# Between layers 1 and 2 of a four-layer Flamingo network: where constants load, in which order the last expert tiles, the sums, the norms and the keys stand

## The chip, the cores and the metric

The kernel runs on one core of one Trainium2 chip. The time is that of one execution on the device, in microseconds (us); the kernel before takes 2595.01 us as the median of three runs (2593.57 to 2595.51). The engines are TensorE (PE; its weight loads are PEld), VectorE (DVE), ScalarE (ACT), GpSimd (POOL) and SyncE (SP, which here only issues transfers).

## What is computed

A batch of 8 sequences of 256 tokens, 512 channels each, float32, goes through four layers. Each layer is `x = x + tanh(g_xattn) * attention(norm(x))`, then `x = x + tanh(g_ffn) * ffn(norm(x))`; attention and FFN are others in each layer. The change lies where layer 1's FFN ends and layer 2's attention begins. Cut to these:

```python
# layer 1, FFN: 64 experts of hidden width 176, 8 of them for each token, and a shared MLP
topk_idx, topk_w = _route(x, router_weight, e_bias)
moe_out = _moe_experts(x, topk_idx, topk_w, w_gate, w_up, w_down)
out = moe_out + _silu(x @ sh_gate) * (x @ sh_up) @ sh_down

# layer 2, attention over channels (per sequence: q = norm(x), k = v = ctx)
scaled = jnp.einsum('bsd,bse->bde', q, k) / sqrt(512)
attn = jax.nn.softmax(scaled, axis=1)
out = jnp.einsum('bde,bse->bsd', attn, v)

# layer 2, FFN: dense, hidden width 2048
h = gelu(x @ proj1.T + proj1_bias)
out = h @ proj2.T + proj2_bias

# layer 3, attention: a scan over time with w = -exp(time_decay), u = time_first
```

## The kernel before

The 2048 tokens are 16 tiles `xt[0..15]` of 128 tokens by 512 channels, held in SBUF for the whole run; four tiles are a block (`TB` = 4, `NB` = 4 blocks of `BLK` = 512 tokens, two sequences of `S` = 256 each). `KC` = 4 is the number of 128-wide pieces of the channels. The kernel is written with a tile framework: each engine runs its instructions in one fixed order, which a scheduler finds from priorities and dependencies when the kernel is built. `behind(one, other, reason)` (L134) only puts an instruction behind another in that order; it adds no wait. `tc.add_manual_dep` with the class `Sync` adds a real wait. Pools of tiles (`t2`, `bp`, `fp`, `wp`) decide which buffer a load must wait for.

*The end of layer 1's FFN* (`middle`). The experts run as a pipeline over tiles of up to 128 gathered token rows (`experts1`, L1421): for each tile the gate and up products, `turn` (L1354: the hidden values are transposed on TensorE and copied back, 128 columns by VectorE, L1360, 48 by ScalarE, L1361), `down` (L1401: the products `ed` with the expert's down weights, a part of 128 rows from `w` and a remainder of 48 rows from `wd`), and an indirect transfer by POOL that adds the result to the tokens' rows in DRAM (L1374, a scatter). There are three such accumulators (`SUMS1` = 3, `acc`). `down` takes two tiles at a time, so that their remainders lie side by side on TensorE. Behind the last tile all five engines load a count (`needing`, L1497) into a register and branch on it (`tc.If`, L1500): the block under it handles experts with too many tokens and isn't run with these inputs. Behind the branch `shared1` (L1157) makes the shared MLP of the last block (tiles 12 to 15): products `shg`, `shu`, `shr` (the gate's and up's remaining 48 columns), Silu on ScalarE, `shT` as two halves (L1174, L1180), and the products `shd`. `combine` (L1522) loads the three accumulators of a tile from DRAM (`more<-acc`, 256 KB each, on SP) and adds them to `xt` on VectorE (L1535). `hidden` holds the VectorE instruction behind which the first tiles' sums are put.

*Layer 2* (`back`). b1 and gb2 (bias rows), and later, behind `xattn2(0)` in the program, constants of layer 3 (`wkv_constants`, L1649: `td`, `tf`, and `w` as an Exp on ScalarE; `place_of`, `run`, `gw` and some more, L1906 to L1949) are loaded and made without a place in the order, so that the scheduler puts them right behind the branch. `L1889` to `L1951` set up: for each of the two sequences of block 0 the sums (`combine`), the load of its keys (`load_kx`, `kxvs`), the norm of its two tiles (`norm_of`: statistics on VectorE, L160 and L163, the root on POOL, L169, the result on VectorE, L179). Behind the first norm stand the four additions of `shd` to tiles 12 to 15 (`last_adds`). `emptied` (L1758) writes empty tables for layer 3. `xattn2` (L1552) makes for each sequence four score products (`s`), a maximum (L1568), Exp (`E`, L1570) and the scaling of the values (L1574), then the products `o` and their addition to `xt`. `step` runs pieces of work for later blocks between these; `ready2` (L1600) makes the norm and the transposes (`tr_f`, copied to `xnT_f` by VectorE L105 and ScalarE L107) for the FFN between the products of the second pair of sequences. `ffn2` (L1618) makes `h2p` (first products, 4 tiles by 4 rounds), Gelu (L1634), and `o2f`; in its first round POOL adds the bias row to `xt` (L1637). Its weights `p` come as 64 tiles of 512 KB on SP.

*The order of transfers on SP* is fixed as well: a load that waits for its buffer holds up all that stand behind it.

## Time and profile before

| | us |
|---|---|
| median of 3 runs | 2595.01 (2593.57 to 2595.51) |
| profiled execution, its time | 2596.3 |
| its span (first to last instruction) | 2594.4 |
| TensorE busy | 2447.8 (94%) |
| VectorE / ScalarE / GpSimd busy | 1276.5 / 643.6 / 902.3 |
| mean granted TensorE clock | 0.979 |
| last expert products end (L1410) | 1409.2 |
| shared products begin (shg) | 1412.56 |
| last scatter issued / first load of a sum | 1412.05 / 1420.78 |
| first scores of layer 2 / second sequence's | 1435.86 / 1447.67 |
| last `o` product of block 1 ends | 1496.87 |
| `h2p`, first product of layer 2's FFN, begins | 1502.58 |

All times within an execution are counted from the start of its span. The views used below: the page's list of busy times; windows (busy time of each engine in a stretch, the clock that TensorE was granted there, and the share and rate of the DMA engines); and timelines of one engine, in which each row gives start, duration, engine, line, operation, `out<-in`, shape, count, and in brackets how long the engine stood idle before it and what ended the wait. A name with q behind it (ACTq, SPq) is the engine's queue: issues of transfers, branches, register work.

### The profile page before, as it was taken

The page shows a single profiled execution, that of the slowest core. Times are in us where ns is not written, and L with a number is a line of the kernel's source. Part 1 is how long each engine was busy: PE and PEld are TensorE (multiplying, and loading weights), DVE is VectorE, ACT ScalarE, POOL GpSimd, SP SyncE. Part 2 cuts the span into 40 slices and gives each one's busy share as a digit, 9 for nine tenths or more (in the row PEclk, how much of TensorE's full clock was granted, in tenths as well). Part 3 has the DMA queues.
Part 4 walks back from the last instruction along what each step waited for, and adds up shares of the span by engine and source line. Part 5 has one row for each costly group of instructions (what it writes and reads, how often), then busy time and mean ns, then how long its engine had stood idle before and what let it go on. Part 6 is the DMA issues. An engine that isn't in the chain of part 4 may idle for free. (4 is left out here: it accounts for less than half of the span.)

```text
span 2594.4 us, 29853 instructions
## 1 busy us (share of the span) xinstructions
PE 2447.8 (94%) x10389; PEld 1258.2 (48%) x10404; DVE 1276.5 (49%) x3517; ACT 643.6 (25%) x1451; POOL 902.3 (35%) x843
## 2 busy tenths in 40 slices
PE   7889898999999999999998999898999999999997
PEld 3444454446655545455554344444444444555553
DVE  7656665645656642222222932768676675111111
ACT  1533444401111122223222211222223122111110
POOL 1110201021355356566664010332424252444442
PEclk9999999989999999999999999999999999999999
DMA  5000010021312149999996822021121212898984
GB/s 223 5 21 21 21 38 9 4 68 49 83 33 66 45 147 255 245 288 267 287 241 129 280 94 105 23 100 57 65 98 65 110 17 49 272 293 291 307 295 81
DMA packets 102179, 333.75 MB, mean 129 GB/s; under 512 B 23287, under 2 KB 25720, under 8 KB 93826
## 3 DMA queue, kind: packets, MB, share of 16 engines
q0 software_dynamic: 48256, 148.74, 21.8%
q1 hardware_dynamic: 50354, 178.73, 19.7%
q10 hardware_dynamic: 3408, 4.25, 0.5%
q8 instruction: 87, 1.43, 0.2%
q14 instruction: 74, 0.61, 0.1%
HBM read 283.35 MB, written 66.88 MB: 135 GB/s over the span
## 5 line engine op out<-in xcount | busy, mean ns | idle before, releaser
L1339 PE MATMUL gu<-w,eb 128*128 128x352 f32 (+1 forms) x1064 | 239.0, 461 | 5.1 <-DMA w<-in_w 4.2
L216 PE MATMUL h2p<-xnT_f,p 128*128 128x512 f32 x512 | 227.1, 598 | 5.7 <-issue 4.4
L216 PE MATMUL o2f<-p,h 128*128 128x512 f32 x512 | 226.0, 595 | 3.3 <-ACT h L1634 3.2
L1374 POOL DMA_INDIRECT acc<-eb,who x94 | 147.4, 1568 | 133.4 <-DVE eb L105 105.3
L546 ACT ACTIVATE pr<-pr,n 128x256 f32<-128x256 f32 x256 | 127.9, 501 | 150.3 <-DVE n L541 145.3
L1339 PEld LDWEIGHTS gu<-w,eb 128*128 128x128 f32 (+1 forms) x1064 | 129.1, 159 | 73.5 <-issue 19.3
L1012 POOL DMA_INDIRECT table<-pay,rowi x128 | 126.0, 984 | 107.0 <-issue 22.3
L216 PEld LDWEIGHTS h2p<-xnT_f,p 128*128 128x128 f32 x512 | 97.1, 192 | 123.4 <-issue 118.5
L216 PEld LDWEIGHTS o2f<-p,h 128*128 128x128 f32 x512 | 95.8, 190 | 122.5 <-issue 114.6
L1391 POOL DMA_INDIRECT xg<-xnd,who x94 | 99.4, 1057 | 46.0 <-PE ehp L1359 19.3
L227 DVE SCALAR_TENSOR_TENSOR x<-o2f,tg,x 128x512 f32<-128x512 f32 x64 | 46.9, 741 | 125.4 <-PE o2f L216 123.9
L598 POOL TENSOR_TENSOR y<-y,gbo 128x512 f32<-128x512 f32 x16 | 20.4, 1274 | 247.0 <-DVE y L597 239.5
L169 POOL TENSOR_TENSOR rstd_a<-ve_a,mhalf 128x4 f32<-128x4 f32 x15 | 15.6, 1043 | 257.7 <-DVE ve_a L167 257.7
L1990 PE MATMUL g_r<-w3gu,xgT 128*128 128x352 f32 (+1 forms) x336 | 102.5, 467 | 0.7 <-ACT xgT L107 0.7
L541 DVE CUSTOM_DVE_ANT_0 pr<-s,mask 128x256 f32<-128x256 f32 x256 | 96.7, 416 | 11.2 <-PE s L521 6.7
L1990 PE MATMUL u_r<-w3gu,xgT 128*128 128x352 f32 (+1 forms) x336 | 100.0, 459 | 0.0
L1999 DVE SCALAR_TENSOR_TENSOR h_r<-a_r,share,u_r 128x352 f32<-128x352 f32 x33 | 19.1, 580 | 161.1 <-PE u_r L1990 157.7
L1634 ACT ACTIVATE h<-h2p,b 128x512 f32<-128x512 f32 x64 | 43.4, 686 | 213.5 <-PE h2p L216 213.3
L2016 PE MATMUL d_r<-w3d,hT_r 128*128 128x512 f32 (+3 forms) x252 | 96.1, 596 | 0.0
L553 PE MATMUL pt<-ident,pr 128*128 128x128 f32 x512 | 86.3, 288 | 9.8 <-ACT pr L546 5.8
L1410 PE MATMUL ed<-w,eb 128*128 128x512 f32 (+1 forms) x266 | 91.2, 601 | 0.9 <-DVE eb L1360 0.9
L553 PEld LDWEIGHTS pt<-ident,pr 128*128 128x128 f32 x512 | 60.1, 144 | 64.9 <-issue 29.1
(587 smaller groups left out, 4685.4 us busy)
## 6 DMA issues: line engine op xcount, KB each, us to landing
w<-in_w SPq DMA_DIRECT2D x64, 960.0 KB, 8.2
p<-in_p SPq DMA_DIRECT2D x64, 512.0 KB, 4.9
acc<-xnd SPq DMA_DIRECT2D x48, 256.0 KB, 5.8
more<-acc SPq DMA_DIRECT2D x48, 256.0 KB, 3.6
xnd<-xn_f SPq DMA_DIRECT2D x32, 256.0 KB, 3.9
wd<-in_wd SPq DMA_DIRECT2D x64, 96.0 KB, 8.2
ctxTa<-in_ctxT SPq DMA_DIRECT2D x4, 1024.0 KB, 6.2
x<-in_x SPq DMA_DIRECT2D x16, 256.0 KB, 5.9
```

What stands on the lines that cost most here:

```text
L216: one = nc.tensor.matmul(ps, lhsT[k], rhs[k], start=(k == 0), stop=(k == n - 1))
L227: return nc.vector.scalar_tensor_tensor(xt[i], ps, scale, xt[i], ALU.mult, ALU.add)
L541: one = nc.vector.tensor_tensor_reduce(pr[:, nt, :], ps[r][:, nt, :], mask[:, nt, :], -1.0, -LOW, ALU.add, ALU.min, n16[:, nt, h : h + 1],)
L546: nc.scalar.activation(pr[:, nt, :], pr[:, nt, :], AF.Exp, bias=n16[:, nt, h : h + 1], scale=-1.0, accum_out=s16[:, nt, h : h + 1],)
L553: nc.tensor.transpose(pt_ps[:, lt, nt, :], pr[:, nt, ts(lt, P)], ident)
L1012: one = nc.gpsimd.indirect_dma_start(out=table[:, :], out_offset=bass.IndirectOffsetOnAxis(ap=rows, axis=0), in_=choice, in_offset=None, b ...
L1339: one = nc.tensor.matmul(gu[part, 0 : 2 * I1], xT[:, k, part], e.gu[:, k, :], start=(k == 0), stop=(k == KC - 1))
L1374: one = nc.gpsimd.indirect_dma_start(out=acc[0][:, :], out_offset=bass.IndirectOffsetOnAxis(ap=index[:stop, col : col + 1], axis=0), in_=s ...
L1391: nc.gpsimd.indirect_dma_start(out=xg, out_offset=None, in_=xnd[:, :], in_offset=bass.IndirectOffsetOnAxis(ap=who[:, col : col + 1], axis= ...
L1410: one = nc.tensor.matmul(ps[n][part, :], t.hT[rows, k, part], wd, start=(k == 0), stop=(k == 1))
L1990: one = nc.tensor.matmul(ps[part, 0:I3], xTt[:, k, part], wgu[k][:, g, :], start=(k == 0), stop=(k == KC - 1))
L2016: one = nc.tensor.matmul(ps[part, :], hT[:cn, n, part], wd[n][:cn], start=(n == 0), stop=(n == 2))
```

## The change

1. The count for the branch is loaded right behind the gather of the experts' table (near 950 us) instead of ahead of the branch.
2. The last two expert tiles' down products are made one by one, the first of them ahead of the last tile's turn.
3. b1, gb2, `td`, `tf`, `gw`, the Exp for `w`, gb2's scaling, `place_of` and the clearing of `run` are put behind the last addition that `xattn2` had made (`pinned`), which moves them to the transposes ahead of layer 2's FFN. On ScalarE two loads of function tables (Exp, Silu) vanish with it.
4. Tile 0's three sums stand behind the first half of `shT`, ahead of the second half; tile 1's behind the second half.
5. Tile 3's three sums are made by GpSimd, with a wait for the first norm's result; its three loads go to one tile of `fp`.
6. Of the four additions of `shd` only two (tiles 14 and 15) stand behind the first norm; tiles 12 and 13 get theirs behind `xattn2(0)`.
7. Tile 2's sums, the second norm, the sums of tiles 4 to 7, the load of block 1's context and both loads of its keys become steps of `xattn2(0)`; `emptied` comes behind `xattn2(1)`. In the order that is built, SP's queue has tile 4 to 7's loads right behind `ctxT` of block 0, then `ctxT` and both keys of block 1, then the three empties.

```diff
@@ -128,5 +128,5 @@
 
-    def columns(key, n, name):
+    def columns(key, n, name, placed=lambda one: one):
         t = sm.tile([P, n], F32, tag="col" + str(n), name=name)
-        nc.scalar.dma_start(t, a[key])
+        placed(nc.scalar.dma_start(t, a[key]))
         return t
@@ -142,5 +142,5 @@
 
-    def row(key, name):
+    def row(key, name, placed=lambda one: one):
         t = sm.tile([P, C], F32, tag=name, name=name, bufs=1)
-        nc.scalar.dma_start(t, a[key].partition_broadcast(P))
+        placed(nc.scalar.dma_start(t, a[key].partition_broadcast(P)))
         return t
@@ -1173,3 +1173,5 @@
                 pu = products("shu", slice(P, 2 * P))
-                nc.vector.tensor_tensor(hT[0], pu, act[0], ALU.mult)
+                one = nc.vector.tensor_tensor(hT[0], pu, act[0], ALU.mult)
+                if later is not None:
+                    hidden[:] = [one]
                 yield
@@ -1182,2 +1184,4 @@
                     )
+                    if later is not None and n == 0:
+                        behind(one, hidden[0], "the first tokens' sums first")
                 hidden[:] = [one]
@@ -1249,3 +1253,5 @@
 
-            def turned_table(name):
+            some = []
+
+            def turned_table(name, meanwhile=None):
 
@@ -1265,2 +1271,4 @@
                     )
+                if meanwhile is not None:
+                    some.append(meanwhile(load))
                 ps = tr.tile([P, 2, P], F32, tag="tr", name=f"who_ps{name}")
@@ -1272,3 +1280,12 @@
 
-            who_ps, one = turned_table("")
+            def needed(load):
+                loads, loaded = nc.values_load_multi_w_load_instructions(
+                    needing[0:1, 0:1], min_val=0, max_val=E1, bass_reorder=False,
+                    skip_runtime_bounds_check_because="a count of 64 experts",
+                )
+                for one in loads:
+                    behind(one, load, "the table's choices first")
+                return loaded[0]
+
+            who_ps, one = turned_table("", needed)
             turned.append(one)
@@ -1462,4 +1479,6 @@
                 n = len(stream)
+                if n % 2 == 0:
+                    down(tiles[n - 2 : n - 1])
                 tiles[n - 1].turn()
-                down(tiles[n - 2 + n % 2 : n])
+                down(tiles[n - 1 : n])
 
@@ -1496,6 +1515,3 @@
             experts1(stream, later=join)
-            some = nc.values_load(
-                needing[0:1, 0:1], min_val=0, max_val=E1, skip_runtime_bounds_check_because="a count of 64 experts"
-            )
-            with tc.If(some > 0):
+            with tc.If(some[0] > 0):
                 again_ps, _ = turned_table("again")
@@ -1514,5 +1530,7 @@
             end = shared1(NB - 1, again, last_adds)
-            for _ in range(3):
+            for _ in range(2):
                 next(end)
-            first_loads.append(combine(range(2), adds=hidden, pool=b8))
+            combine(range(1), adds=hidden, pool=b8)
+            next(end)
+            first_loads.append(combine(range(1, 2), adds=hidden, pool=b8))
             for _ in end:
@@ -1648,7 +1666,7 @@
 
-    def wkv_constants(lp):
-        td = columns("td3", KC, "td3")
-        u = columns("tf3", KC, "tf3")
+    def wkv_constants(lp, pinned):
+        td = columns("td3", KC, "td3", pinned)
+        u = columns("tf3", KC, "tf3", pinned)
         w = lp.tile([P, KC], F32, tag="w3", name="w3")
-        nc.scalar.activation(w, td, AF.Exp)
+        pinned(nc.scalar.activation(w, td, AF.Exp))
         nc.vector.tensor_scalar(w, w, -1.0, None, ALU.mult)
@@ -1746,4 +1764,2 @@
             l3 = early.enter_context(tc.tile_pool(name="l3", bufs=1, side="right", reuse_waits=REUSE))
-            b1 = columns("b1_2", HID // P, "b1_2")
-            gb2 = gated_row("b2_2", 6, "gb2")
             dp = st.enter_context(tc.tile_pool(name="m3d", bufs=1, space=DRAM))
@@ -1861,3 +1877,3 @@
 
-            rest = []
+            rest, passed = [], []
 
@@ -1865,2 +1881,4 @@
 
+                if behind is not None:
+                    passed[:] = [behind]
                 for _ in range(n):
@@ -1888,2 +1906,6 @@
 
+            def pinned(one):
+                behind(one, passed[0], "layer 2's first scores first")
+                return one
+
             xns = []
@@ -1891,16 +1913,53 @@
                 tiles = (2 * bb, 2 * bb + 1)
-                loaded = combine(tiles, kx_load) if bb else first_loads.pop()
+                loaded = combine(tiles[:1], kx_load) if bb else first_loads.pop()
+                if bb:
+                    more = fp.tile([P, KC, C], F32, tag="b8", name="more3")
+                    for u in range(SUMS1):
+                        one = nc.sync.dma_start(more[:, u, :], results[u][ts(3, P), :])
+                        behind(one, loaded, "not before it in the queue")
+                        loaded = one
+                        add = nc.gpsimd.tensor_tensor(out=xt[3], in0=xt[3], in1=more[:, u, :], op=ALU.add)
+                        if u == 0:
+                            tc.add_manual_dep(
+                                add.ins,
+                                other.ins.name,
+                                mybir.DependencyInfo(mybir.DependencyClass.Sync, mybir.DependencyReason.DATA),
+                                reason="the first tokens' norm first",
+                            )
                 kxvs[bb] = load_kx(bb, bp, loaded)
-                xns += norm_of(tiles, f"a2{bb}_")
-                other = latest_norm[0]
-                for add in last_adds:
-                    behind(add_scaled(*add), other, "layer 2's first tokens first")
-                last_adds.clear()
+                if bb == 0:
+                    xns += norm_of(tiles, "a20_")
+                    other = latest_norm[0]
+
+            def second_half():
+
+                for stats in stats_of((2, 3), "a21_"):
+                    yield
+                xns.extend(normed(stats, "a21_"))
+                yield
+                for t in range(TB, 2 * TB):
+                    loaded = combine((t,))
+                    yield
+                context(1, loaded)
+                for b in range(2, 4):
+                    kxvs[b] = load_kx(b, bp, loaded)
+                yield
+
+            for add in last_adds[2:]:
+                behind(add_scaled(*add), other, "layer 2's first tokens first")
             context(0, loaded)
             first_loads.append(loaded)
-            emptied()
-            loaded = combine(range(TB, 2 * TB))
-            context(1, loaded)
+            rest.append(second_half())
+            more_adds = last_adds[:2]
+            last_adds.clear()
             xattn2(0, xns, (bp, fp), step)
-            wkv = wkv_constants(l3)
+            step(1000)
+            for add in more_adds:
+                pinned(add_scaled(*add))
+            xattn2(1, norm(1, "a2"), (bp, fp), step, ready2(0, fp, None))
+            emptied()
+            b1 = columns("b1_2", HID // P, "b1_2", pinned)
+            gb2 = row("b2_2", "gb2", pinned)
+            pinned(nc.vector.tensor_scalar(gb2, gb2, tg[:, 6:7], None, ALU.mult))
+            wkv = wkv_constants(l3, pinned)
             before = lp.tile([P, P], BF16, tag="before3", name="before3")
@@ -1930,4 +1989,4 @@
             place_of = lp.tile([P, 2], F32, tag="place_of3", name="place_of3")
-            nc.vector.tensor_scalar(place_of[:, 0:1], part, -float(FULL3), None, ALU.add)
-            nc.vector.tensor_scalar(place_of[:, 1:2], part, float(FULL3), None, ALU.is_lt)
+            pinned(nc.vector.tensor_scalar(place_of[:, 0:1], part, -float(FULL3), None, ALU.add))
+            pinned(nc.vector.tensor_scalar(place_of[:, 1:2], part, float(FULL3), None, ALU.is_lt))
             nc.vector.scalar_tensor_tensor(
@@ -1943,3 +2002,3 @@
             nc.gpsimd.memset(gw, 0.0)
-            nc.scalar.dma_start(gw[:, :, 0:8], a["gwT3"].rearrange("p (k e) -> p k e", k=KC))
+            pinned(nc.scalar.dma_start(gw[:, :, 0:8], a["gwT3"].rearrange("p (k e) -> p k e", k=KC)))
 
@@ -1948,5 +2007,4 @@
             run = lp.tile([P, TT + 1, 8], BF16, tag="run3", name="run3")
-            nc.vector.memset(run[:, 0, :], 0.0)
+            pinned(nc.vector.memset(run[:, 0, :], 0.0))
             row_i = lp.tile([P, TT, 2], I32, tag="row3", name="row3")
-            xattn2(1, norm(1, "a2"), (bp, fp), step, ready2(0, fp, gb2))
 
```

More of the change, by code (lines that the diff above doesn't have):

```diff
@@ L1899, in back @@
+            for add in last_adds[2:]:
+                behind(add_scaled(*add), other, "layer 2's first tokens first")
             context(0, loaded)
             first_loads.append(loaded)
+            rest.append(second_half())
+            more_adds = last_adds[:2]
+            last_adds.clear()
+            xattn2(0, xns, (bp, fp), step)
+            step(1000)
+            for add in more_adds:
+                pinned(add_scaled(*add))
+            xattn2(1, norm(1, "a2"), (bp, fp), step, ready2(0, fp, None))
@@ L1901, in back @@
             emptied()
-            loaded = combine(range(TB, 2 * TB))
-            context(1, loaded)
-            xattn2(0, xns, (bp, fp), step)
-            wkv = wkv_constants(l3)
+            b1 = columns("b1_2", HID // P, "b1_2", pinned)
+            gb2 = row("b2_2", "gb2", pinned)
+            pinned(nc.vector.tensor_scalar(gb2, gb2, tg[:, 6:7], None, ALU.mult))
+            wkv = wkv_constants(l3, pinned)
             before = lp.tile([P, P], BF16, tag="before3", name="before3")
```

## Prediction

> **What bounds the kernel now.** I read the page's busy table first:
>
> ```profile
> PE   2447.8 (94%) x10389; PEld 1258.2 (48%) x10404; DVE 1276.5 (49%) x3517; ACT 643.6 (25%) x1451; POOL 902.3 (35%) x843
> ```
>
> TensorE bounds the whole, so only its idle time and its slow clock can be won. The windows of 20 us around the layer border show where both lie; columns are busy time (instructions) of each engine, granted clock, DMA share, GB/s:
>
> ```profile
> 1380.00:1400.00 20.00, 20.00 (x84) 11.67 (x83) 5.56 (x14) 6.56 (x16) 8.42 (x6) 1.00 0.57 86
> 1400.00:1420.00 20.00, 15.78 (x41) 6.73 (x40) 2.27 (x5) 2.49 (x7) 6.19 (x4) 0.91 0.45 66
> 1420.00:1440.00 20.00, 14.79 (x33) 5.40 (x32) 13.38 (x28) 5.24 (x6) 3.30 (x18) 0.91 0.81 267
> 1440.00:1460.00 20.00, 17.03 (x40) 7.34 (x40) 19.44 (x53) 5.51 (x15) 0.69 (x1) 1.00 0.75 256
> 1480.00:1500.00 20.00, 17.96 (x54) 8.48 (x52) 19.10 (x43) 4.24 (x10) 7.38 (x5) 1.00 0.85 303
> 1500.00:1520.00 20.00, 17.42 (x35) 7.67 (x36) 8.56 (x20) 4.08 (x6) 1.02 (x1) 0.83 0.09 36
> ```
>
> Some 17 us of 1400 to 1520 are idle on TensorE, and VectorE is full from 1440 to 1500. TensorE's timeline places the idle time (start, length, product, count, [idle before, releaser]):
>
> ```profile
> 1408.07 1.13 PE L1410 MATMUL ed<-wd,eb 48*128 48x512 f32 x4
> 1412.56 5.22 PE L216 MATMUL shg<-xnT_f,shgu 128*128 128x512 f32 x8 [3.36 <-ACTq L1500]
> ...
> 1427.28 6.02 PE L1192 MATMUL shd<-shd,shT 128*128 128x512 f32 x16 [2.64 <-DVE shT L1174]
> 1435.86 1.86 PE L216 MATMUL s<-xn_a__0_13383,kxvs 128*128 128x512 f32 x2 [2.57 <-DVE xn_a__0_13383 L179]
> ...
> 1447.67 1.10 PE L216 MATMUL s<-xn_a__0_13422,kxvs 128*128 128x512 f32 x2 [2.97 <-ACT E L1570]
> ...
> 1498.33 1.09 PE L194 MATMUL tr_f<-ident,xn_f 128*128 128x128 f32 x8 [1.46 <-DVE xnT_f L105]
> 1502.58 16.57 PE L216 MATMUL h2p<-xnT_f,p 128*128 128x512 f32 x32 [3.16 <-issue]
> ```
>
> Six gaps: the branch, shT, the first norm, the second norm, and two ahead of the FFN (h2p). After h2p TensorE has no gap, so the start of h2p is the mark that moves the end. ScalarE's timeline says why shT is late, and POOL's what ScalarE waited for:
>
> ```profile
> 1422.42 0.64 ACTq L1944 DMA_DIRECT2D gw<-in_gwT  x1
> 1423.09 1.28 ACT L1653 ACT_TABLE_LOAD   x1 [13.24 <-DVE place_of L1933]
> 1424.39 0.20 ACT L1653 ACTIVATE w<-td 128x4 f32<-128x4 f32 x1
> 1424.61 1.28 ACT L1171 ACT_TABLE_LOAD   x1
> 1425.90 0.60 ACT L1171 ACTIVATE sha<-shg 128x512 f32<-128x512 f32 x1
> ```
>
> ```profile
> 1412.05 1.55 POOL L1374 DMA_INDIRECT acc<-eb,who  x1 [0.30 <-issue]
> 1421.09 0.20 POOL L1907 MEMSET before<- 128x128 bf16 x1 [7.50 <-DMA acc<-eb,who]
> ```
>
> The releaser named for the table load, a VectorE operation, stands for the issue of gw: that waits for POOL, and POOL for the last scatter. So shg, finished by 1417.8, gets its Silu at 1425.9. VectorE's timeline then:
>
> ```profile
> 1426.53 0.69 DVE L1174 TENSOR_TENSOR shT<-shu,sha 128x512 f32<-128x512 f32 x1 [1.74 <-DMA gw<-in_gwT]
> 1427.26 0.88 DVE L1180 TENSOR_TENSOR shT<-sha,shr 48x256 f32<-48x256 f32 x2
> 1428.16 2.75 DVE L1535 TENSOR_TENSOR x<-x,more 128x512 f32<-128x512 f32 x4
> ...
> 1498.20 3.68 DVE L1535 TENSOR_TENSOR x<-x,more 128x512 f32<-128x512 f32 x6
> ```
>
> The norm's sums stand behind both shT, and six sums of later tiles (1498.20) ahead of the copy that h2p needs.
>
> **The change, part by part.** *Last two expert tiles one by one.* Now 1405.22 ed92, 1406.18 turn, 1407.04 ed93, 1408.07 the four remainders, end 1409.20. Two remainders (about 0.57) move ahead of the last turn, which then starts at 1406.94. VectorE now has the result of ed92 (0.69) to copy ahead of the turned hidden values (0.29): done 1408.1, ScalarE's small copy 1408.4. From there 0.85 and 1.1 for ed93: end 1410.25, **+1.05**. Tile 92's scatter leaves sooner, hidden.
>
> *The load of the count.* Five loads (PE 0.87, DVE 0.54, ACT 0.47, POOL 0.51, SP 0.27) go from ahead of the branch to behind the table's gather near 950 us, where TensorE waits 1.09 for the table's rows anyway; I cost them at 0 (0 to 0.5 if ACT's and DVE's delay the token list). At the branch, ScalarE's last copy ends 1410.9 instead of 1409.85, but the branch no longer stands behind its 0.47. In the trace the ScalarE branch took 2.7 from 1409.8 to its event at 1412.5, and shg followed. So shg starts about 1413.1, **+0.5** (1412.1 if TensorE's own branch, 3.66, can start earlier; 1414 if the copy counts in full).
>
> *Constants later.* b, gb, td, tf, gw, Exp, two table loads and seven small VectorE and POOL operations leave the stretch. Silu then follows shg at once, and shT half 0 follows shu. The last scatter is issued at 1411.15 (0.9 earlier: one tile's copy is ahead of it, and no count is loaded). It landed 7.3 after issue, beside the constants' packets; the stage's median is 6.8, its least 4.8. I take 5.5, nearest the row of the scatter before it (5.7). With the 1.43 from landing to first load, `more` is issued at 1418.1 instead of 1420.78.
>
> *First tile's sums between the shared products.* With T = 1413.1: shr ends at T+12.1 as now (1424.64 less 1412.56), with its Silu (0.6) and two shT operations (0.88) at T+13.65. Tile 0's three sums and statistics (2.5) fit before that: its third load lands near 1422.8. shd needs half 1 only after its first four of 16 products (1.5), so its 2.64 gap goes; it runs to T+18.2. Behind half 1 there stand three sums (1.85), statistics (0.85), rstd on POOL with its handover (1.0), xn (0.9): T+18.3. First scores at T+18.6 = 1431.7, before 1435.86: **-4.2**. The next gap falls from 2.57 to 0.4.
>
> *Half the sums on GpSimd, two last sums away.* Between the first xn and the second VectorE loses tile 3's three sums (1.8) and the two of shd (1.3), which go behind the fourth scores. What is left is 7.3 by its spacing (0.60 a sum, reduce or statistic, 0.66 an addition of shd), and the rstd handover: second scores at 1440.85, before 1447.67, **-6.8**. POOL's 128x512 two-input rows are 1.27 (L598) and 1.5 (four of L1637 in 6.00), so three are 3.9 to 4.5: done 1436, ahead of the statistics that wait for them. But beside POOL's L1637 VectorE's xn took 0.96 each (four in 3.83) against 0.48 (four in 1.92 at 1507.81), and a sum 1.09 against 0.68. Half of POOL's stretch at such rates adds 1.2: s1 at 1442, **-5.7**. I take -6.0, where POOL's own additions are nearest; by the free and the fully doubled rate it is -6.8 and -3.0.
>
> [...]
>
> *Keys first.* From second scores to the end of the last o product TensorE ran 49.2 without a gap (1447.67 to 1496.87). Block 1's keys, kxvs2 and kxvs3, now go out right behind tile 7's loads, ahead of `table` and `p`; kxvs3 went out at 1467.19, behind loads that waited for buffers, and its scores did not wait for it, so this alone gains 0. VectorE in that stretch has 31 sums and ten longer additions instead of 35 and seven, so it is 0.5 shorter; being 98% busy, it sets the pace. I keep 49.2. On SP's queue three empties (for layer 3) and p (512 KB, 4.9 to land, first needed at h2p) stand behind the keys.
>
> *Constants beside the transposes.* POOL's four additions (6.00) no longer lie beside xn_f, since gb lands later; xn_f falls from 3.83 to 1.92. With the sum of 1.09 back at 0.6, the first copy ends 2.1 to 2.9 sooner; from there to the second copy five sums and two additions stand instead of six sums, 0.7 more. Last product to h2p: 3.5 to 4.3, I take 3.7 instead of 5.7, **-2.0** (0 if POOL was not what slowed xn_f, so that only the 0.7 and the fewer waits are left; -2.2 at best). The Exp for layer 3 holds ScalarE until td lands (b and gb took 4.3 and 6.0), ahead of the first Gelu; but h2p has 16 us of products before o2f needs the last Gelu, so 10 us stand over. Cost 0.
>
> The sum: -6.0 and -2.0 = **-8.0** at h2p. Profiled time 2596.3 (span 2594.4 and 1.9 around it) to 2588.3; that run stands 1.3 over the median shown, so the median goes to 2587.0.
>
> **Rivals.** *The clock also comes back at h2p.* The 32 products of h2p took 16.57, those of the next round 13.9; the granted clock was 0.60 and 0.72 in 1500 to 1510, behind idle gaps of 1.46 and 3.16. Yet behind 2.64 it stayed at 1.00 (1425 to 1430), and behind 2.57 it fell to 0.66 (1435 to 1440): a gap of about 3 can go either way. If it stays, another 2.7: -10.7, 2584.3. [...] Chance 0.18.
>
> *GpSimd stands in VectorE's way* (above): -3.0 at s1, -2.0 at the tail: -5.0, 2590.0. For: xn_f at double length. Against: sums slowed only 1.6 times. Chance 0.20.
>
> *Transfers bind.* DMA share was 0.75 to 0.85, with stretches at 1.0. If tile sums wait for loads, only the earlier first load counts: -2.7, 2592.3. Against: SP's loads waited for buffers (VectorE 14.1 us) more than for data. Chance 0.12.
>
> *The shared remainder behind tile 0's sums, slower.* Now shT half 1, and so shd, wait for tile 0's loads and thereby for the last scatter. First scores come at 1424.7 plus the landing. At 5.5 that is covered; at the stage's longest, 10.3, scores gain 0.9; with what VectorE and the tail save, it is even near 14; at 18 the kernel is 4 slower (2599). No landing seen reaches it. Chance 0.05.
>
> **How the numbers follow.** Forecast 0.45, of -6.5 to -9.5. The likeliest case gives 2587.0. 0.2% is 5.2 us, about what a measurement of this kernel can tell from no change. Faster by more: 0.45 + 0.18 + under half of the GpSimd case, 0.08 = 0.71; same: the rest of it, the transfers and part of the last, 0.25; slower 0.04. The range leaves out the last rival and the ends of the clock and transfer cases: 2582.5 to 2592.5.
>
> **What would show it.** Right: shg near 1413, Silu right behind it, no Exp ahead of it; shd without a gap; first scores near 1431.7, second near 1441.5; h2p near 1494.5 (1502.58 now). Wrong: a gap of shd put down to shT L1182; statistics of tile 3 waiting for POOL; sums of 1 us in 1431 to 1436; TensorE gaps "<-DMA more" in 1440 to 1490; a gap ahead of o2f "<-ACT h" after td. A scatter that lands after 10 us, or a tail that stays at 5.7, breaks the sum.

## The result, and the profile after

The changed kernel takes 2589.86 us (median of 22 runs, 2585.1 to 2596.3), the kernel before in the same comparison 2594.2 (22 runs, 2591.07 to 2598.09). The ratio is 0.9984, 95% interval 0.9978 to 0.9991: 4.2 us less (2.3 to 5.7). On two other chips, compared there with the kernel before, the same program gave 0.9981 (0.9967 to 0.9994) and 0.9979 (0.9965 to 0.9993). So the change makes the kernel faster, by about half of the 8.0 that was forecast and less than the 5.2 that the prediction had called the limit of a measurement. By the prediction's own chances, a gain of more than 0.2% had 0.71; the 0.16% measured lies in what it counted as the same, 0.25. The profiled execution took 2589.42, its span 2587.7.

The page's list of busy times, and the windows of 20 us around the layer border (busy time and instructions of PE, PEld, DVE, ACT, POOL; granted clock, DMA share, GB/s):

```profile
PE 2446.7 (95%) x10389; PEld 1254.9 (48%) x10404; DVE 1274.6 (49%) x3514; ACT 641.4 (25%) x1449; POOL 906.5 (35%) x846
```

```profile
1400.00:1420.00 20.00, 15.06 (x31) 5.91 (x30) 1.49 (x4) 2.02 (x5) 6.94 (x18) 0.83 0.64 123
1420.00:1440.00 20.00, 16.99 (x42) 6.41 (x40) 17.54 (x35) 4.20 (x8) 5.88 (x5) 1.00 0.78 286
1440.00:1460.00 20.00, 19.13 (x42) 8.52 (x43) 17.77 (x46) 3.80 (x11) 1.33 (x4) 0.91 0.60 212
1480.00:1500.00 20.00, 17.43 (x49) 8.41 (x48) 17.22 (x38) 1.65 (x5) 4.12 (x3) 0.91 0.91 325
1500.00:1520.00 20.00, 20.00 (x48) 8.92 (x47) 7.63 (x17) 4.03 (x5) 4.06 (x4) 1.00 0.02 3
```

TensorE is busy for 5.6 us more of these five stretches than before (88.6 instead of 83.0). But look at the clock column: 0.83, 1.00, 0.91, 0.91, 1.00, where the kernel before had 0.91, 0.91, 1.00, 1.00, 0.83. The mean is 0.93 in both; the slow clock has not grown, it has moved. TensorE's timeline shows where to, and what ended the waits:

```profile
1405.73 1.12 PE L1427 MATMUL ed<-wd,eb 48*128 48x512 f32 x2
1410.80 6.45 PE L216 MATMUL shg<-xnT_f,shgu 128*128 128x512 f32 x8 [3.94 <-ACTq L1516]
1417.08 3.60 PE L216 MATMUL shu<-xnT_f,shgu 128*128 128x512 f32 x8
1420.51 3.60 PE L216 MATMUL shr<-xnT_f,shgu 128*112 128x512 f32 x8
1423.95 5.91 PE L1196 MATMUL shd<-shd,shT 128*128 128x512 f32 x16
1430.47 1.13 PE L216 MATMUL s<-xn_a__0_13378,kxvs 128*128 128x512 f32 x2 [0.61 <-DVE xn_a__0_13378 L179]
...
1440.87 2.04 PE L216 MATMUL s<-xn_a__0_13442,kxvs 128*128 128x512 f32 x2 [3.27 <-ACT E L1588]
1442.71 1.50 PE L216 MATMUL s<-xn_a__1_13444,kxvs 128*128 128x512 f32 x2
...
1491.27 1.04 PE L194 MATMUL tr_f<-ident,xn_f 128*128 128x128 f32 x8
1494.88 15.66 PE L216 MATMUL h2p<-xnT_f,p 128*128 128x512 f32 x32 [2.57 <-issue]
```

The gap ahead of shd is gone, that ahead of the first scores is 0.61, and last `o` product to h2p is down to 3.4. But the gap at the branch grew from 3.36 to 3.94, shg takes 6.45 where shu, the same work, takes 3.60, and the first pair of the second scores takes 2.04 instead of 1.10. (The 3.27 ahead of them is put down to ScalarE's E, which had ended by 1440.0; what came last is VectorE's second norm, xn from 1440.23 to 1440.78.) ScalarE, POOL and VectorE did what the change meant them to: Silu right behind shg, tile 0's sums ahead of shT's second half, tile 3's on POOL:

```profile
1417.33 0.60 ACT L1171 ACTIVATE sha<-shg 128x512 f32<-128x512 f32 x1 [9.85 <-PE shg L216]
1424.20 0.59 ACT L1179 ACTIVATE sha<-shr 48x512 f32<-48x512 f32 x1 [6.27 <-PE shr L216]
```

```profile
1407.75 1.54 POOL L1391 DMA_INDIRECT acc<-eb,who  x1 [1.50 <-ACT eb L107]
1414.40 0.20 POOL L1966 MEMSET before<- 128x128 bf16 x1 [5.10 <-DMA acc<-eb,who]
...
1430.95 4.76 POOL L1921 TENSOR_TENSOR x<-x,more 128x512 f32<-128x512 f32 x3 [1.12 <-DVE xn_a__1_13380 L179]
```

```profile
1421.38 2.13 DVE L1553 TENSOR_TENSOR x<-x,more 128x512 f32<-128x512 f32 x3
...
1424.82 0.88 DVE L1182 TENSOR_TENSOR shT<-sha,shr 48x256 f32<-48x256 f32 x2 [0.36 <-ACT sha L1179]
...
1430.90 1.41 DVE L227 SCALAR_TENSOR_TENSOR x<-shd,tg,x 128x512 f32<-128x512 f32 x2
1432.23 2.36 DVE L1553 TENSOR_TENSOR x<-x,more 128x512 f32<-128x512 f32 x2
1434.51 0.68 DVE L1586 TENSOR_REDUCE m<-s 128x1 f32<-128x512 f32 x1
1435.11 1.15 DVE L1553 TENSOR_TENSOR x<-x,more 128x512 f32<-128x512 f32 x1
```

Ahead of all this the two executions already differ by 3.7 us: the next-to-last expert tile's first product (ed92) starts at 1405.22 before and at 1401.52 after. 2.6 of these arise before 950, where both programs are the same. So marks are counted from ed92 below. In these traces a float32 product of h2p, shd or the scores is two rows (the kernel makes 16 for a round of h2p, which stand as x32); where the text counts h2p's 32, shd's 16 or the scores' 16, it counts rows.

| from ed92, us | before, 2 executions | forecast | changed, 4 executions |
|---|---|---|---|
| last expert product ends | 3.98, 3.97 | 5.03 | 5.33 to 5.34 |
| shg begins | 7.34, 7.26 | 7.88 | 9.28, 8.84, 9.29, 9.25 |
| start of shg to start of shu | 5.05, 6.62 | 5.05 | 6.28, 6.37, 5.16, 5.64 |
| first scores | 30.64, 30.18 | 26.5 | 28.95, 28.60, 27.84, 28.28 |
| second scores | 42.45, 41.99 | 36.5 | 39.35, 39.02, 38.26, 38.69 |
| their 16 products, to the first `o` | 6.94, 6.94 | 6.94 | 8.33, 8.35, 6.94, 6.94 |
| h2p begins | 97.36, 96.92 | 89.4 | 93.36, 93.06, 90.89, 91.31 |
| o2f begins | 113.76, 113.37 | 105.8 | 108.85, 108.56, 106.40, 106.82 |

The second execution before is e1, those of the changed kernel are e2, e5 and e10. The third and fourth are from the other two chips; both kernels take some 45 us longer there, which in the traces arises between 650 and 980, ahead of all that is compared.

### The profile page after: what moved, and what is told of

It is laid out like the page before. It is cut to its first block, busy times and chain, and to the rows that moved or that the text cites. A ratio compares the mean times of both kernels' runs of the same rounds, so it can differ in the third digit from the quotient of the medians.

```text
span 2587.7 us, 29852 instructions
## 1 busy us (share of the span) xinstructions
PE 2446.7 (95%) x10389; PEld 1254.9 (48%) x10404; DVE 1274.6 (49%) x3514; ACT 641.4 (25%) x1449; POOL 906.5 (35%) x846
## 5 line engine op out<-in xcount | busy, mean ns | idle before, releaser
L1408 POOL DMA_INDIRECT xg<-xnd,who x94 | 99.5, 1058 | 44.9 <-issue 18.6
```

The lines of the kernel that those rows point to most:

```text
L1408: nc.gpsimd.indirect_dma_start(out=xg, out_offset=None, in_=xnd[:, :], in_offset=bass.IndirectOffsetOnAxis(ap=who[:, col : col + 1], axis= ...
```

## The experiments

**Theory A**: the steps behind the branch went as forecast, but the branch takes longer and TensorE's clock, lost in the gaps that remain, now lies on the path. **Rival B**: GpSimd's sums in VectorE's way, or transfers, ate the front's gain.

**e1 and e2: both kernels once more.**

> The kernel before once more, for how much its own marks vary. Counted from the first product of the next-to-last expert tile (ed92), shg began at 7.34, the first scores at 30.64, the second at 42.45, h2p at 97.36, o2f at 113.76. Theory A (TensorE's clock and the branch are part of the forecast's miss): shg's 5.22 and h2p's 16.57 are draws of the clock and may differ by 1 to 2 here, the other marks by under 0.5. Theory B (GpSimd's sums or the transfers took the missing part): all marks come back within 0.5, o2f at 113.3 to 114.3.

> The changed kernel once more. Its marks from ed92: shg 9.28 (lasting 6.45), first scores 28.95, second 39.35, last o product's end 89.7, h2p 93.36, o2f 108.85. Theory A: shg takes between 3.6 and 6.5 and the second scores' 16 products between 6.9 and 8.4 as the clock falls out, and the gap ahead of shg is 3 to 4; the sums of VectorE beside GpSimd's stay at 1.15. Theory B: shg and the scores' products take what they took, and the distance from first to second scores stays at 10.4.

Measured: the marks of the table. The kernel before kept all marks within 0.5 but shg's length (5.05 and 6.62). The changed kernel came back within 0.45 everywhere, its slow shg (6.28, 6.37) and slow second scores (8.33, 8.35) too; the one execution each took 2594.55 and 2593.29. On the other two chips the loss fell out otherwise (5.16 and 5.64; 6.94 and 6.94), with all else the same. So the same program can have the loss or not. Whether the chip, the state at the start or chance decides, one or two executions of each can't tell.

**e3: remainders side by side again.**

```diff
-                if n % 2 == 0:
-                    down(tiles[n - 2 : n - 1])
                 tiles[n - 1].turn()
-                down(tiles[n - 1 : n])
+                down(tiles[n - 2 + n % 2 : n])
```

> The changed kernel with the last two expert tiles' remainders side by side again, as before. Theory A: in the changed kernel nothing waited for the last scatter any more (tile 0's sums began right behind shT half 0 at 19.86 from ed92, the loads had been issued at 12.56), while every us ahead of the branch counts; so expert products end 1.35 earlier, shg begins 1.2 earlier, first scores 1 earlier, and the time falls by 1 to 1.3. Rival (the earlier scatter of the next-to-last tile is needed): sums wait for loads, first scores are the same or later, and the time is 0 to 1 longer.

Measured: expert products end at 3.98, shg begins at 6.69 and shr ends 3.7 earlier than in the changed kernel. But the last scatter leaves at 6.84 instead of 6.23, the loads go out at 13.83 instead of 12.56, and then, in TensorE's and VectorE's timelines:

```profile
1425.60 7.37 PE L1196 MATMUL shd<-shd,shT 48*128 48x512 f32 x12 [3.52 <-DVE shT L1182]
```

```profile
1423.45 0.69 DVE L1551 TENSOR_TENSOR x<-x,more 128x512 f32<-128x512 f32 x1 [4.09 <-DMA more<-acc]
```

Tile 0's third load is late, shT's second half stands behind its sum, shd waits for that: the wait that the prediction's last rival named. First scores 31.42, o2f 110.60, later than the changed kernel. Most of that lateness is the clock, to judge by the products behind the wait: these 12 rows of shd took 7.37, where the same 12 took 4.55 in e9 and all 16 took 5.91 in the changed kernel, and the first norm's result was there at 29.2. The measured ratio, 0.9960 (0.9947 to 0.9974), says the opposite, and its interval lies below the changed kernel's. The profiled execution was the slowest of the five (2590.39, median 2587.22), so the stall need not be in the others, and only one execution of the changed kernel was timed beside these (e2, 2593.29). What side by side does to the time stays open; it may be that this part of the change costs time. That the two edits hang together (sums ahead of shT's half wait for the later scatter) is shown by this trace.

**e4: idle products in the gaps.**

```diff
+            fill(16, "branch")        # matmul(ident, ident), 128x128, not read
             with tc.If(some[0] > 0):
...
+            if blk == 0 and bb:
+                fill(6, "scores")
```

> The changed kernel with 16 idle products (identity by identity, 128x128, result not read) behind the last expert product, ahead of the branch, and six ahead of the second scores. Nothing else moves. Theory A: with TensorE busy in the branch's gap shg runs in 3.6 to 4.2 instead of 6.45, first scores come 2 to 2.5 earlier; the second scores' products take 6.9 instead of 8.3; in all 2.5 to 4 less. Theory B: shg gets faster, but first scores wait for loads or VectorE, second scores stay at 39 from ed92, time the same within 1. Should the branch wait until TensorE's queue is empty, shg begins 1 to 2 later and half of the gain goes.

Measured: the second scores' products took 6.94. Ahead of the branch it failed:

```profile
1410.05 3.84 PE L226 MATMUL fill_branch<-ident 128*128 128x128 f32 x32
1418.51 5.93 PE L216 MATMUL shg<-xnT_f,shgu 128*128 128x512 f32 x8 [4.62 <-issue]
```

TensorE's compare came at 1411.7, when most of the idle products had been issued, took 3.4 (3.3 to 4.1 in the other runs), and 3.3 more followed for which the trace names no other engine ("issue"). A transfer of 16 KB of instructions lies in them (1415.85 to 1417.16), so the engine was probably still fetching the instructions behind the branch; no run tests it. shg began 4.45 later than in the changed kernel, and slow again. o2f 111.42; ratio 0.9983 (0.9974 to 0.9992). The branch was not hidden but moved.

**e5: the changed kernel, timed beside e6 to e8.**

> The changed kernel, timed on the same chip as the three that follow, so that they can be compared with it. o2f at 108.5 to 109 from ed92, the stretch ahead of it (start to ed92) anywhere from 1401 to 1406 as in the runs so far; time 3 to 8 under the kernel before. Both theories alike.

Measured: ratio 0.9981 (0.9967 to 0.9994), o2f 106.40, under the expected 108.5: neither theory had said so, and it is the clock (shg 5.16, second scores 6.94 at full speed).

**e6: the constants alone, on the kernel before.** Only item 3 of the change.

> The kernel before with only the constants moved (b1, gb2, td, tf, gw, Exp, place_of, run to the transposes ahead of layer 2's FFN). Theory A (the constants held up Silu and the scatter, the rest of the change gives back what it brings ahead of the branch): shT follows shu and shr at once, no gap ahead of shd, first scores at 28 to 29 from ed92 (30.2 to 30.6 before, 28.6 to 28.95 in the changed kernel), second scores at 40 to 41 (VectorE still has tile 3's sums and four shd additions), h2p 3.7 behind the last o product, o2f at 109 to 110.5: most of the changed kernel's 5. Rival (the order of the sums and GpSimd bring the gain): first scores not before 30, o2f at 112 or later.

Measured: no gap ahead of shd, first scores at 28.68, second at 40.49, h2p at 94.78, o2f at 110.28; ratio 0.9992 (0.9979 to 1.0004), which can't be told from the kernel before. TensorE's timeline:

```profile
1469.27 5.91 PE L1192 MATMUL shd<-shd,shT 128*128 128x512 f32 x16
1478.76 2.08 PE L216 MATMUL s<-xn_a__0_13378,kxvs 128*128 128x512 f32 x2 [3.57 <-DVE xn_a__0_13378 L179]
```

As A expected: first scores come as early as in the whole change (27.84 to 28.95), with a gap of 3.57 left ahead of them. In the changed kernel the sums' order has closed that gap to 0.61, but shd ends 2.1 to 3.2 later there (25.11 here), by the tiles one by one, the branch and the clock behind it. By its marks the constants alone bring 3.1 to 3.5 at o2f of the change's 4.5 to 7.4; GpSimd, the two last additions and the clock (second scores' products 8.64 here) make the rest.

**e7: tile 3's sums on VectorE.**

```diff
-                        add = nc.gpsimd.tensor_tensor(out=xt[3], in0=xt[3], in1=more[:, u, :], op=ALU.add)
-                        if u == 0:
-                            tc.add_manual_dep(...)
+                        nc.vector.tensor_tensor(xt[3], xt[3], more[:, u, :], ALU.add)
```

> The changed kernel with tile 3's three sums on VectorE, without a wait for the first norm. Theory A (GpSimd helps by about what the sum said): VectorE's sums in 32 to 35 from ed92 take 0.67 instead of 1.15, but three more of 0.6 stand ahead of the second norm: first to second scores 10.4 to 11.2 instead of 10.4; time the same to 1 longer. Theory B (GpSimd in VectorE's way ate the front's gain): first to second scores under 9.5, time 1 to 2 shorter.

Measured: VectorE's sums are back at full speed, and first to second scores takes 11.12 instead of 10.40 to 10.42:

```profile
1477.09 1.41 DVE L1553 TENSOR_TENSOR x<-x,more 128x512 f32<-128x512 f32 x2
```

Two in 1.41, where beside GpSimd two took 2.36. So GpSimd does slow VectorE, by 0.45 to 0.5 for each of three sums, and still gains 0.7. Rival B falls as far as GpSimd goes; for the transfers, no gap of TensorE from the second scores to the last `o` product is left in the changed kernel that a load could have made. The ratio, 0.9996 (0.9982 to 1.0011), overlaps the changed kernel's; behind the longer gap (3.99) the second scores' products took 9.74.

**e8: side by side, shT's half first, and filled scores.** e3 with `combine(range(2), adds=hidden)` behind both halves of shT, and e4's six idle products.

> The changed kernel with the remainders side by side, the second half of shT ahead of tile 0's sums again, and six idle products (identity by identity, result not read) ahead of the second scores. Theory A: expert products end at 4.0, shg begins at 6.7, shr ends at 18.9, shd has no gap and ends at 25; then tile 0's third load (landing near 22) and VectorE's sums set the first scores at 27.5 to 28.5 (28.6 to 28.95 in the changed kernel, 31.4 with side by side alone); the second scores' products take 6.9 instead of 8.4; o2f 106 to 107.5, time 1 to 3 under the changed kernel. Rival (the last scatter, 0.6 later side by side, sets it): first scores at 29.5 or later, time the same.

Measured: shd has no gap any more and ends at 26.21, first scores 29.35: later than expected, since shg took 6.57 and tile 0's first sum came at 22.08. Second scores' products 6.94, h2p's 32 at full clock (13.81), o2f 106.19; ratio 0.9980 (0.9967 to 0.9992), the changed kernel's. For the first scores A was too hopeful by 0.9 to 1.9 and the rival's 29.5 nearly right; o2f lies where A put it.

**e9: the next-to-last scatter held back.** The changed kernel with one wait added: tile 92's scatter waits for ScalarE's copy of tile 93.

> The changed kernel with one more wait and nothing else: the next-to-last tile's scatter is not issued before ScalarE has copied the last tile. So far ScalarE's branch took 2.6 to 2.8 from its compare to its event in the four programs with remainders side by side (and in the one with the constants alone), and 3.4 to 3.9 in those with the tiles one by one. Theory C (instruction fetch behind the scatter's packets, which fly there only one by one): 2.5 to 2.9 here, shg 8.0 to 8.4 from ed92 instead of 8.8 to 9.3, but the first load of a sum comes 1.9 later. Rival D (it is that VectorE branches earlier there, so that the two no longer fetch together): 3.4 to 3.9 as in the changed kernel.

ScalarE's compare at the branch and its event behind it, where it goes on (last column: first and last start), in the changed kernel and in e9:

```profile
L1516 ACTq COMPARE_BRANCH  x1: 50/50/50, 1406.9 to 1406.9; - x1
L1516 ACTq EVENT_SEMAPHORE  x1: 17/17/17, 1410.7 to 1410.7; - x1
```

```profile
L1532 ACTq COMPARE_BRANCH  x1: 50/50/50, 1461.5 to 1461.5; - x1
L1532 ACTq EVENT_SEMAPHORE  x1: 17/17/17, 1464.2 to 1464.2; - x1
```

3.8 against 2.7, and shg at 8.20 instead of 8.84 to 9.29. VectorE's branch is as early in e9 as in the changed kernel (2.6 from ed92 in both), so D falls. The traces also hold the transfers of instructions. In the 2.1 us behind ScalarE's compare all DMA queues carried (packets, MB, share), in the changed kernel and in e9:

```profile
q0 software_dynamic: 129, 0.24, 85.9%
```

```profile
q14 instruction: 1, 0.01, 0.9%
```

The first is the scatter; the first packet of instructions leaves 2.2 after the compare, when the scatter's packets have gone (1.8 to 2.2 in all six executions with that scatter ahead of the compare). In e9 it leaves after 1.2; in the five with the scatter behind the compare, where VectorE branches beside ScalarE, the first two leave after 0.9 and 1.2. So ScalarE's branch is slower in the changed kernel by about the 1.0 by which its instructions come later, behind the packets of the scatter sent just ahead of it: e9 holds that scatter back, and both differences are nearly gone. e9 is one execution (2643.15) and pays for the quick branch: its first load of a sum goes out at 14.69 instead of 12.3 to 12.6.

**e10 to e12: the shared products ahead of the branch.** e10 is the changed kernel once more. In e11 shg, shu, their Silu and shT's first half stand ahead of the branch; e12 adds 12 and six idle products.

```diff
+            end = shared1(NB - 1, again, last_adds)
+            for _ in range(2):
+                next(end)
             with tc.If(some[0] > 0):
...
-            end = shared1(NB - 1, again, last_adds)
-            for _ in range(2):
-                next(end)
-            combine(range(1), adds=hidden, pool=b8)
             next(end)
-            first_loads.append(combine(range(1, 2), adds=hidden, pool=b8))
+            first_loads.append(combine(range(2), adds=hidden, pool=b8))
```

> The changed kernel, timed on the same chip as the two that follow. o2f at 106 to 109 from ed92, as the clock falls out; time 3 to 6 under the kernel before.

> The changed kernel with the shared products shg and shu, their Silu and the first half of shT ahead of the branch (they read nothing that the experts make), their two buffers in one tile of b8, and the second half of shT ahead of tile 0's sums. Theory A (the branch and the cold clock behind it cost what the forecast missed): TensorE has 6.9 of products to run while it fetches, the gap of 3.6 to 3.9 ahead of shg goes, shg and shu run at full clock; shr begins at 12 to 14 from ed92, shd ends at 22 to 23.5 (28 now). From there loads and VectorE set the first scores, 26.5 to 27.5 (28.6 to 28.95 now, 27.8 with a lucky clock); o2f 105 to 107, time 1.5 to 3 under the changed kernel. Rival (the sums wait for the last scatter, which is the bound): first scores at 28.5 or later, and the time the same; the gap only moves to ahead of the first scores.

> As the one before, with idle products (identity by identity, result not read): 12 ahead of the first scores (2.8) and six ahead of the second. Theory A: first scores at the same place as without, but both scores' 16 products at full clock, 6.9 each (8.3 to 8.6 where the clock was lost); o2f 1.4 to 2.8 earlier than without if the clock was lost there, the same if not. Rival (the clock's window, not the length of the gap, decides, and idle products of half the gap don't help): one of the two still takes over 8.

Measured: e10 0.9979 (0.9965 to 0.9993), o2f 106.82. e11 0.9970 (0.9957 to 0.9983), o2f 105.47. e12 0.9954 (0.9936 to 0.9973), o2f 104.00, 9.4 to 9.8 under the kernel before. TensorE in e11, then in e12:

```profile
1455.60 3.60 PE L216 MATMUL shu<-xnT_f,shgu 128*128 128x512 f32 x8
1460.18 3.66 PE L216 MATMUL shr<-xnT_f,shgu 128*112 128x512 f32 x8 [0.99 <-DVEq L1526]
...
1474.59 2.08 PE L216 MATMUL s<-xn_a__0_13377,kxvs 128*128 128x512 f32 x2 [5.00 <-DVE xn_a__0_13377 L179]
```

```profile
1464.23 2.94 PE L226 MATMUL fill_scores<-ident 128*128 128x128 f32 x24
1468.78 1.12 PE L216 MATMUL s<-xn_a__0_13377,kxvs 128*128 128x512 f32 x2 [1.61 <-DVE xn_a__0_13377 L179]
```

The branch's gap is 0.99 instead of 3.9, shg's eight rows run between the last tiles' products, at full clock (1.02 to 1.13 for two), and shd ends at 20.96 (27.2 to 28.3). A's marks came or were passed: shd ends before its 22, and the first scores come before its 26.5, at 25.96. But the rival's mechanism is there too: a gap of 5.0 now stands ahead of the first scores, since the sums wait for the last scatter, and of the 6.3 to 7.4 that shd gained 1.9 to 3 are left. Behind that gap a pair takes 2.08; with e12's idle products the first scores come at 25.44 and at full clock (1.12 a pair), the second 1.5 earlier than in e11. e12 is ahead of both kernels by its medians on that chip (2628.19; e11 2631.94; changed 2635.08; before 2641.0); its interval overlaps those of e11 and of the changed kernel, so against these two the gain is likely, not shown.

## Why the prediction was right, and where it was not

The time lies in the range, the sign is right, and the gain is half. The likeliest case (-6.5 to -9.5, chance 0.45) did not come. The range holds the result because it was drawn over several rivals; the one nearest in number, GpSimd's -5.0, is not the reason, and no rival named the branch. That part is luck. By its steps, each from ed92:

- **Last tiles one by one, +1.05**: measured +1.35. The last tile's products began where forecast (3.16; 3.1 to 3.2), but their first part took 1.05, not 0.85; the rows of before had 1.03 for it (1407.04 to 1408.07).
- **shg +0.5**: measured +1.5 to +2.0. This step failed. It took ScalarE's 2.7 at the branch for fixed, and called the earlier scatter "hidden"; that scatter makes the branch 3.4 to 3.8 (e9). Taking away the count's load (0.47) is in it and cannot pay for that. The last scatter's landing was put well: 4.6 and 4.9 where it was seen (5.5 taken), the first load at 12.3 to 12.6 (12.9).
- **First scores at T+18.6**: 19.67, 19.76, 18.55, 19.03. The order was right: Silu behind shg, no gap ahead of shd, tile 0's sums in time. The step carried over shg's 5.05 from a trace in which shg's slowness was hidden (shd waited for shT anyhow). Now 1.7 to 2.9 of shg's time, against 3.43 at full clock, lie on the path. With the branch: first scores -1.7 in the two profiled executions, not -4.2.
- **Second scores 10.0 later**: 10.40 to 10.42. GpSimd's three sums took 4.76 (3.9 to 4.5 forecast), VectorE's beside them 1.15 to 1.18. The latter is the forecast's sign "sums of 1 us in 1431 to 1436", which it had listed as wrong, though its own -6.0 had 0.8 of that cost in it. Measured are 1.4 for the three sums (1.7 times their length), and the step came out 0.4 long. The doubled rate behind the -3.0 no run shows for sums.
- **Second scores to the last product, 49.2 kept**: 50.57, 50.59, 49.18, 49.18. Where the clock stayed, the step is exact; where it fell behind the gap of 3.27, 1.4 more. The prediction asked whether the clock returns at h2p; it did not ask where else it might go.
- **Tail 3.7**: 3.44 to 3.45, with xn_f at 1.91 as forecast; and h2p's products took 15.5 instead of 16.4, 0.9 of the 2.7 in the clock rival.
- **Keys first, count's load, Exp's wait**: 0 as forecast. td held ScalarE until 1499.42, and o2f followed h2p without a gap.

The sum for the profiled pair: 0.3 + 1.1 + 1.1 + 0.4 + 1.4 - 0.3 = 4.0 is missing at h2p, and -8.0 became -4.0 (-6.5 and -6.1 from the first execution before in e5 and e10, where the clock held better). Summed the other way: take the clock's excess on the path out of each stretch to o2f (before 2.6 at h2p; changed 2.85 + 1.39 + 1.69, in e5 1.73 + 0 + 1.7), and the change shortens it by 8.2 in both. That 8.2 is near 8.0 by chance: the forecast carried 1.6 of shg's slowness along, so on the same footing it was -9.6. The 1.4 that are missing are the last tile's 0.3, the branch's 1.1 and GpSimd's 0.4, less 0.3 at the tail and 0.1 at the first scores. Most of the work was found; the clock took 3.3 or 0.8 of it back.

The prediction also says that TensorE has no gap after h2p. It has: ahead of the `o` products of layer 2's next two blocks it waits 5.5 to 5.7 each in both kernels. From o2f to the end the kernel before took 1075.4 and 1076.5, the changed one 1077.3, 1076.9, 1077.6 and 1076.4. In the first three of these four the `o` products behind the first such gap run 1.25 slower than before, and those behind the second 1.0 faster (12.07 to 12.13, before 13.09 and 13.10); in the fourth both are as before. So the clock's loss moves there too (in the two profiled executions the `o` products behind the first gap have a clock of 0.50 for 5.7, before for 3.1), and only 0.2 to 0.4 of the later difference is explained by it; the rest stays open.

The slower sums that the GpSimd rival named are there and cost little (1.4 for the three); the transfers did not bind; the late scatter's wait came in e3, when its cover was taken away, not here.

## What to carry to other kernels

When a gap goes, ask what else was hidden in it: a slow product in front of a wait costs nothing until the wait is gone. The branch here cost ScalarE 2.6 to 3.8 us, and its instructions came 1 us later behind a scatter's packets (2.2 against 1.2 after the compare), so put work that doesn't depend on a branch ahead of it, enough for the engine to run meanwhile (in e11 the gap fell from 3.9 to 0.99), and don't send a transfer just before. Where a short gap cannot be closed, try a few idle products in it: in the four gaps ahead of scores that were filled so, TensorE kept its clock (6.94 for the second scores' 16 products, 1.12 for e12's first pair). When a forecast carries a length over from a trace, ask whether that length was on the path there.

## What the runs showed of the hardware

**Where the clock fell, it stood at half.** Windows cut to the stretches of low clock (busy time of PE, clock, DMA share, GB/s), changed kernel:

```profile
1409.50:1412.90 3.40, 2.10 (x3) 0.51 0.53 70
1412.90:1416.30 3.40, 3.40 (x5) 0.50 0.27 89
1416.40:1419.80 3.40, 3.40 (x9) 1.00 0.94 303
1436.90:1440.20 3.30, 0.70 (x2) 1.00 1.05 405
1440.30:1443.70 3.40, 2.83 (x4) 0.50 0.08 28
1443.80:1447.20 3.40, 3.40 (x9) 1.00 0.58 170
```

A clock of 0.50 to 0.51, for one or two stretches of 3.4 each, and 1.00 right behind them; the stretches that are full or nearly full of work lost 1.4 to 1.7 each. Behind idle gaps of 1.9 (e6's second scores, 8.64) to 3.9 (shg above) it came or did not come (e10's second scores, behind 3.28, took 6.94). Two executions of one program (the profiled one and e2), at 4.6 us apart, lost the clock at the same products and to within 0.1 us. What decides whether it falls behind a gap, no run here shows. All three executions with six idle products ahead of the second scores (e4, e8, e12) kept 6.94; of the nine executions without, in kernels with the constants moved, five lost 1.4 to 2.8 there and four kept it. That speaks for the idle products and does not prove them.

**The jump over the block that is left out took 2.6 to 4.1, and its price moved.** From ScalarE's compare to its event it took 2.6 to 2.9 where a scatter's packets had nearly gone or had not yet come, and 3.4 to 3.8 where they flew right behind the compare (a scatter issued 2.2 ahead of it); TensorE's took 3.3 to 4.1 in all. The traces hold transfers of instructions behind the compare. The first of their packets left 1.8 to 2.2 after ScalarE's compare where the scatter's packets flew, 0.9 after it where they had not yet come, and 1.2 in e9, where the branch took 2.7 instead of the changed kernel's 3.8.

**Beside GpSimd only some of VectorE's operations were slower.** Beside its three sums VectorE's sums of two SBUF operands took 1.15 to 1.18 instead of 0.68, while the reduction (0.68) and the additions with one operand in PSUM (0.70) kept their times. An operation with a single tensor operand was slower as well: in the kernel before, the norm's result xn_f, whose one tensor operand is in SBUF, took 0.96 each beside GpSimd's additions (four in 3.83), and in the changed kernel, without them, 0.48 (four in 1.91).
